# A changed order of steps, and one store for two, at the end of a post-norm attention and feed-forward block

## The chip, the core and the metric

The kernel runs on one core of a Trainium2 chip. The core has a matrix engine (TensorE, PE in the profile), a vector engine (VectorE, DVE), an engine for pointwise functions (ScalarE, ACT), a general one (GpSimd, POOL) and one that mainly starts transfers (SyncE, SP). Each has its own stream of instructions; they wait for each other through semaphores. Transfers run on 16 DMA engines and are started from the streams of SP, ACT or POOL. The metric is the time of one execution on the device in microseconds (us), the median over runs.

## What is computed

4096 tokens of width 256 go through two halves, each followed by a layer norm of the sum with its input:

```python
def _layernorm(x, axis=-1, eps=1e-05):
    m = jnp.mean(x, axis=axis, keepdims=True)
    v = jnp.var(x, axis=axis, keepdims=True)
    return (x - m) / jnp.sqrt(v + eps)

x = L0_attn_x                                   # (1, 4096, 256)
x = _layernorm(x + attention(x))                # linear attention, width 64
x = _layernorm(x + ffn(x))

# ffn: w1, w2 256 -> 1024, h1, h2 1024 -> 1024, w3 1024 -> 256; tlin(x, w, s) = (x @ w.T) * s
h = silu(tlin(x, w1, s1)) * tlin(x, w2, s2)
h = gelu(tlin(h, h1, hs1)); h = gelu(tlin(h, h2, hs2))
return tlin(h, w3, s3)
```

The change is in the very last layer norm, for the last 256 tokens.

## The kernel before

The tokens are cut into eight tiles of 512 (NT = 8); a tile is four groups of 128 tokens (NS = 4), one token to a partition. Tiles are worked on in pairs. Products are made from two roundings of each float32 operand, a high part and a low part, so every weight block is multiplied twice. TensorE runs the products of the feed-forward layers one after the other for the whole program.

The schedule is written by hand: the order of the calls in the source is the order of the instructions on each engine. The framework adds the semaphores.

The kernel takes a short way that holds only for certain weights and variances. While it runs, it gathers tests of that: `differ` compares weights, `within` (lines 1003 to 1006) tests that each group's variance lies between `low` and `high`. At the end all tests are reduced to one number, `flag`. PE, ACT, DVE and SP load it (line 1219), and branch on it (line 1225): where the flag is set, `general` computes everything again in plain float32; otherwise the program ends. On these inputs the branch skips it.

The end of the program, after the last products (lines 1152 to 1225), handles the last pair of tiles, `ta` and `tb`. For each group: `scaled` (line 891) multiplies the product in PSUM by s3 on VectorE, a sum adds it to the residual in `x2`, `bn_stats` and `bn_aggr` on VectorE give mean and variance into `mvo`, a reciprocal root is formed, and the group is normed and stored. The early groups take their root from GpSimd (`rstd_of`, line 84) and are normed by two ScalarE instructions (`norm_on_act`).

The last two groups of `tb`, 2 and 3, are done otherwise. `root_on_act` (line 1133) takes the square root on ScalarE, adds epsilon to the variance on VectorE, and returns four small VectorE steps: a reciprocal and one Newton step in three instructions. In the kernel before, the lines from 1190 run as follows. Group 2: statistics (by `statistics`), root, minus mean, and its subtraction on ScalarE (line 1195). Then VectorE has group 3's scaled product (1196), and group 2's four steps with group 3's sum (1198), statistics (1201) and aggregate (1204) among them. ScalarE scales group 2 (1205), and SP stores it (1206, 128 KB). Group 3: its root (1207), the range tests of `tb` (1208), and its four steps with the minimum over all tests (1210), TensorE's 1x1 product that sums it over the partitions (1213) and the comparison that makes `flag` (1216) among them. VectorE norms group 3 in one instruction (1217), SP stores it (1218, 128 KB), and the flag is loaded.

Of the kernel before, what the change touches and what calls it, by code (L numbers as in the profile page):

```python
# [11 lines left out]
F32 = mybir.dt.float32  # L12
# [3 lines left out]
AF = mybir.ActivationFunctionType  # L16
ALU = mybir.AluOpType
# [4 lines left out]
P = 128  # L22
# [22 lines left out]
def block_kernel(ctx: ExitStack, tc: tile.TileContext, a: dict, out: bass.AP):  # L45
# [15 lines left out]
    nc = tc.nc  # L61
# [3 lines left out]
    def const(name, shape, dt=F32):  # L65
        return cp.tile(shape, dt, tag=name, name=name)

    s1 = const("s1", [P, KH])
# [13 lines left out]
    flag = const("flag", [1, 1], I32)  # L82
# [14 lines left out]
    p2 = fast.enter_context(tc.tile_pool(name="two", bufs=2))  # L97
# [24 lines left out]
    x2 = {}  # L122
# [24 lines left out]
    def norm_stats(us, mv, s0):  # L147
        st = p2.tile([P, 2, 6], F32, tag="bn", name="bn")
        for j, u in enumerate(us):
            nc.vector.bn_stats(st[:, j, :], u)  # L150
        for j in range(len(us)):
            nc.vector.bn_aggr(mv[:, s0 + j, :], st[:, j, :])
# [331 lines left out]
    def sums(layer, k, raw):  # L484
# [20 lines left out]
        def first():  # L505
            plus(v[0], a21, a22)
            plus(v[1], v[0].bitcast(F32), a11, ALU.subtract)
            store(0)

        def second():  # L510
            plus(v[2], a11, a21, ALU.subtract)
            plus(v[3], a12, v[1].bitcast(F32), ALU.subtract)
            store(1)
# [23 lines left out]
    for c in (slice(0, H // 2), slice(H // 2, H)):  # L537
        d = nc.gpsimd.dma_start(out=w1[:, :, c], in_=a["w1"][:, :, c])
# [237 lines left out]
    for i in range(2, 2 * KH):  # L776
# [13 lines left out]
        if i in (11, 14):  # L790
            t = 2 + i // 14
# [86 lines left out]
    mvo = p1.tile([P, NT * NS, 2], F32, tag="mvo", name="mvo")  # L878
# [12 lines left out]
    def scaled(t, s):  # L891
        ps = (al, be)[t % 2][s]
        d = p2.tile([P, E], F32, tag="d", name=f"d{t}", bufs=4)
        nc.vector.tensor_tensor(d, ps[:, :E], s3, ALU.mult)  # L894
        return d
# [28 lines left out]
    def end_jobs(t, engine=nc.gpsimd, queue=nc.gpsimd):  # L924
        root, norm, store = out_norm(t)

        def half(s):
            root([s, s + 1])
            for i in (s, s + 1):
                norm(i, engine)  # L930
            if s:
                store(0, NS, queue)

        return [(1.3, functools.partial(half, s)) for s in (0, 2)]
# [68 lines left out]
    def within(dst, var, so_far):  # L1003

        nc.vector.tensor_scalar(dst, var, low, so_far, ALU.is_ge, ALU.mult)
        nc.vector.scalar_tensor_tensor(dst, var, high, dst, ALU.is_le, ALU.mult)
# [20 lines left out]
    for p in range(NP):  # L1027
        ta, tb = 2 * p, 2 * p + 1
        if p > 0:
            first = []  # L1030
            ask(1)
            for i in range(2 * KH):
# [13 lines left out]
                if p + 1 < NP and i in (6, 11):  # L1046
                    t = ta + 2 + int(i == 11)
# [77 lines left out]
    def statistics(t, ss):  # L1125
        norm_stats([x2[t][:, s, :] for s in ss], mvo[:, t * NS : (t + 1) * NS, :], ss[0])
# [6 lines left out]
    def root_on_act(t, s):  # L1133

        var, r, e = (p3.tile([P, 1], F32, tag=n, name=n) for n in ("var", "rr", "re"))
        mv = mvo[:, t * NS + s, 1:2]
        nc.scalar.activation(r, mv, AF.Sqrt, bias=eps)
        nc.vector.tensor_scalar(var, mv, EPS, None, ALU.add)


        return r, [
            functools.partial(nc.vector.reciprocal, r, r),
            functools.partial(nc.vector.scalar_tensor_tensor, e, r, var, r, ALU.mult, ALU.mult),
            functools.partial(nc.vector.tensor_scalar, e, e, -0.5, 1.5, ALU.mult, ALU.add),
            functools.partial(nc.vector.tensor_tensor, r, r, e, ALU.mult),
        ]

    def store(t, s0, s1):
        nc.sync.dma_start(out=out[t][:, s0:s1, :], in_=x2[t][:, s0:s1, :])

    g, v = nc.gpsimd, nc.vector
    for s in range(NS):
# [23 lines left out]
    for s in range(2):  # L1176
        norm_on_act(ta, 2 + s, *ra[s])
    store(ta, 2, 4)
    d = scaled(tb, 1)
    statistics(tb, [0])  # L1180
    (r0,) = roots(tb, [0])
    y = x2[tb][:, 1, :]
# [6 lines left out]
    store(tb, 0, 2)  # L1189
    n = (NT - 1) * NS  # L1190
    y, u = x2[tb][:, 2, :], x2[tb][:, 3, :]
    statistics(tb, [2])
    r, steps2 = root_on_act(tb, 2)
    (m,) = minus_mean(tb, [2])
    nc.scalar.activation(y, y, AF.Identity, bias=m, scale=1.0)
    d = scaled(tb, 3)
    steps2[0]()
    v.tensor_tensor(u, u, d, ALU.add)
    steps2[1]()
    st = p2.tile([P, 2, 6], F32, tag="bn", name="bn")  # L1200
    nc.vector.bn_stats(st[:, 0, :], u)
    steps2[2]()
    steps2[3]()
    nc.vector.bn_aggr(mvo[:, n + 3, :], st[:, 0, :])
    nc.scalar.activation(y, y, AF.Identity, scale=r)
    store(tb, 2, 3)
    r, steps3 = root_on_act(tb, 3)
    within(ok[:, n - NS :], mvo[:, n - NS :, 1], fine)
    steps3[0]()
    nc.vector.tensor_reduce(some, ok, AX.X, ALU.min)  # L1210
    steps3[1]()
    pf = bank[7][:1, :1]
    nc.tensor.matmul(pf, some, ones, start=True, stop=True)
    steps3[2]()
    steps3[3]()
    nc.vector.tensor_scalar(flag, pf, float(P), None, ALU.is_lt)
    nc.vector.tensor_scalar(u, u, mvo[:, n + 3, 0:1], r, ALU.subtract, ALU.mult)
    store(tb, 3, 4)
    differs = nc.values_load(
        flag, engines=AGAIN, min_val=0, max_val=1,  # L1220
        skip_runtime_bounds_check_because="0 or 1: a comparison's result",
# [177 lines left out]
```

## Time and profile before

| what | us |
|---|---|
| median of 3 runs | 638.11 (638.07 to 639.05) |
| the profiled execution | 637.49 |
| its span, first to last instruction | 635.6 |
| mean granted TensorE clock | 0.997 of full |

The profile comes from one execution on the chip. Its page gives for each engine the busy time and its share of the span, a picture of the span in 40 slices, the DMA queues, the chain of work that ended last, and groups of like instructions. A row of the timeline has the start in us from the span's start, the duration, the engine, the line of the program, the operation, and what it writes and reads. Engine names with a q (SPq, ACTq) are sequencers: they wait, branch, or start transfers, while the engine itself may be idle. Queue 1 in the DMA views is SP's, queue 0 GpSimd's, queue 10 ScalarE's; queues of kind "instruction" bring program code to the engines.

The stores of the last tiles, as their line 1149 shows them (duration ns least, median, largest; first and last start):

```profile
L1149 SPq DMA_DIRECT2D out<-x x5: 332/333/338, 623.3 to 631.9; - x5
```

The first three are of two groups each (256 KB), the last two of one (128 KB).

### The profile page before, as it was taken

What the parts mean: (1) busy time and instruction counts of PE and PEld (TensorE: products, weight loads), DVE (VectorE), ACT (ScalarE), POOL (GpSimd) and SP (SyncE); (2) the same over time, 40 slices, a digit from 0 to 9 for tenths busy, and PEclk for the clock granted to TensorE, in tenths of its full rate; (3) what the DMA queues carried; (4) which work ended last, traced back from release to release, by engine and by line L of the source; (5) the groups of instructions that cost most, each with busy time, mean ns of one, the idle gap of its engine ahead of it and who ended that gap; (6) DMA issues with size and microseconds to landing.
All of it is one profiled execution on the core that took longest, in us unless ns stands there. A gap on an engine that the chain in (4) does not pass through costs nothing.

```text
span 635.6 us, 9039 instructions
## 1 busy us (share of the span) xinstructions
PE 623.6 (98%) x3169; PEld 526.8 (83%) x3169; DVE 488.0 (77%) x767; ACT 379.1 (60%) x547; POOL 218.0 (34%) x280
## 2 busy tenths in 40 slices
PE   8999999999999999999999999999999999999995
PEld 6778888888898888888898888888898888888895
DVE  2889985889568788789668798798676896597456
ACT  5455452659845374655755457757764547765674
POOL 1333023204855409405545505603653700000043
PEclk9999999999999999999999999999999999999998
DMA  8979669978651168646851135645761035543201
GB/s 345 377 270 320 228 218 360 278 248 244 168 154 67 59 206 276 221 134 215 231 151 33 67 131 185 218 162 173 229 162 35 33 131 171 174 153 132 100 1 69
DMA packets 59409, 113.31 MB, mean 178 GB/s; under 512 B 19776, under 2 KB 34112, under 8 KB 59232
## 3 DMA queue, kind: packets, MB, share of 16 engines
q1 hardware_dynamic: 40880, 73.89, 35.7%
q0 software_dynamic: 18192, 38.41, 19.6%
q8 instruction: 26, 0.43, 0.3%
q10 hardware_dynamic: 288, 0.39, 0.2%
q14 instruction: 23, 0.19, 0.1%
HBM read 96.94 MB, written 18.87 MB: 182 GB/s over the span
## 4 chain that ended last, share of the span: by engine, by line
PE 93%; DMA 3%; DVE 2%; issue 0%; ACT 0%; SPq 0%; POOL 0%; DVEq 0%; POOLq 0%
PE bank L305 64%; PE bank L724 18%; PE bank L885 9%; DMA f<-in_h 2%; PE bank L140 1%; DMA f<-in_xt 1%; DVE so L317 1%; PE bank L210 0%; DVE stk L663 0%; DVE bn L150 0%; PE bank L650 0%; PE bank L734 0%; DVE d L894 0%; PE bank L615 0%; ACT hi L218 0%
## 5 line engine op out<-in xcount | busy, mean ns | idle before, releaser
L305 PE MATMUL bank<-hi,ws 128*128 128x512 f32 x896 | 348.7, 389 | 0.0
L305 PE MATMUL bank<-lo,ws 128*128 128x512 f32 x896 | 348.6, 389 | 0.0
L260 DVE TENSOR_TENSOR lo<-f,hi 128x1024 fp32r<-128x1024 f32 x142 | 168.3, 1224 | 59.5 <-ACT hi L259 59.0
L305 PEld LDWEIGHTS bank<-hi,ws 128*128 128x128 f32 x896 | 168.2, 188 | 34.9
L305 PEld LDWEIGHTS bank<-lo,ws 128*128 128x128 f32 x896 | 168.2, 188 | 34.9
L259 ACT CAST hi<-f 128x1024 fp32r<-128x1024 f32 x142 | 142.6, 1052 | 48.4 <-PE bank L305 25.1
L355 ACT ACTIVATE f<-f,hs 128x512 f32<-128x512 f32 x96 | 62.5, 715 | 68.7 <-DVE f L317 68.7
L724 PE MATMUL bank<-hi,w 128*128 128x512 f32 (+1 forms) x256 | 99.0, 388 | 1.0 <-DVE stk L663 1.0
L724 PE MATMUL bank<-lo,w 128*128 128x512 f32 (+1 forms) x256 | 98.8, 387 | 0.0
L743 ACT ACTIVATE f<-bank,s 128x512 f32<-128x512 f32 x64 | 44.0, 689 | 64.8 <-PE bank L724 60.2
L317 DVE TENSOR_TENSOR f<-f,f 128x1024 f32<-128x1024 f32 x64 | 76.5, 1221 | 4.5 <-ACT f L355 3.8
L317 DVE TENSOR_TENSOR f<-f,bank 128x512 f32<-128x512 f32 x96 | 61.4, 681 | 15.3 <-ACT f L410 11.3
L744 DVE SCALAR_TENSOR_TENSOR f<-bank,s,f 128x512 f32<-128x512 f32 x64 | 47.7, 747 | 24.9 <-PE bank L724 23.8
L885 PE MATMUL bank<-w,lo 128*128 128x256 f32 x240 | 57.9, 283 | 0.0
L885 PE MATMUL bank<-w,hi 128*128 128x256 f32 x240 | 57.9, 283 | 0.0
L724 PEld LDWEIGHTS bank<-hi,w 128*128 128x128 f32 x256 | 48.1, 188 | 10.8 <-DVE stk L663 1.2
L244 POOL DMA_DIRECT2D xT<-x x96 | 52.2, 551 | 14.0 <-DMA stage<-in_h 5.9
L724 PEld LDWEIGHTS bank<-lo,w 128*128 128x128 f32 x256 | 48.1, 188 | 9.5
L847 POOL DMA_DIRECT2D stage<-in_h x16 | 9.2, 575 | 126.6 <-DVE stage L873 96.7
L885 PEld LDWEIGHTS bank<-w,lo 128*128 128x128 f32 x240 | 46.1, 192 | 0.2
L885 PEld LDWEIGHTS bank<-w,hi 128*128 128x128 f32 x240 | 46.0, 192 | 0.2
L410 ACT COPY f<-bank 128x512 f32<-128x512 f32 x32 | 18.6, 589 | 28.6 <-PE bank L305 28.5
(165 smaller groups left out, 544.5 us busy)
## 6 DMA issues: line engine op xcount, KB each, us to landing
ws<-sw SPq DMA_DIRECT2D x100, 512.0 KB, 3.5
sw<-so POOLq DMA_DIRECT2D x16, 512.0 KB, 4.9
stage<-in_h POOLq DMA_DIRECT2D x16, 512.0 KB, 5.5
ws<-in_h POOLq DMA_DIRECT2D x12, 512.0 KB, 6.3
sw<-in_h SPq DMA_DIRECT2D x12, 512.0 KB, 5.6
x<-in_x SPq DMA_DIRECT2D x16, 256.0 KB, 5.2
f<-in_xt SPq DMA_DIRECT2D x7, 512.0 KB, 6.7
f<-in_h SPq DMA_DIRECT2D x6, 512.0 KB, 7.2
```

The lines of the kernel that those rows point to most:

```text
L244: moves.popleft()()
L259: nc.scalar.copy(hi[:, c, :], src[:, c, :])
L260: nc.vector.tensor_tensor(lo[:, c, :], src[:, c, :], hi[:, c, :].bitcast(F32), ALU.subtract)
L305: nc.tensor.matmul(ps[2 * h + o], w[:, k, o * P : (o + 1) * P], part[i][:, k, :], start=start and k == 0 and i == 0, stop=k == HK - 1 and ...
L317: engine.tensor_tensor(dst, u, v, op)
L355: nc.scalar.activation(dst, src, AF.Gelu, scale=sc[:, o : o + 1])
L410: nc.scalar.copy(bb[:, o], al[o])
L724: nc.tensor.matmul(ps[:, c], w[:, k, o * P : (o + 1) * P], part[:, 2 * j + k, c], start=(k == 0 and i == 0), stop=(k == KE - 1 and i == 1),)
L743: nc.scalar.activation(g, pa, AF.Silu, scale=s1[:, o : o + 1])
L744: nc.vector.scalar_tensor_tensor(g, pb, s2[:, o : o + 1], g, ALU.mult, ALU.mult)
L847: nc.gpsimd.dma_start(out=st[:, :n], in_=src.rearrange("p k o -> p (k o)")[:, c : c + n])
L885: nc.tensor.matmul(ps[:, :E], part[q][:, k, s * P : (s + 1) * P], w3[:, k0 + k, :], start=i % 2 == 0 and k == 0 and q == 0, stop=i % 2 == ...
```

## The change

- Group 3's scaled product and sum move ahead of group 2's root, and its statistics ahead of group 2's first small step.
- Group 2's subtraction on ScalarE stays, its scaling now comes after the flag's comparison in the source.
- The range tests, the minimum and the 1x1 product move ahead of most of the small steps; the flag's comparison moves ahead of the last step of group 2 and the last two of group 3.
- The small steps of groups 2 and 3 alternate. Group 2 gets a `bn` buffer of its own in place of that in `statistics`.
- The two stores of 128 KB from SP become one of 256 KB from ScalarE's queue, after both groups are normed.

```diff
-    def store(t, s0, s1):
-        nc.sync.dma_start(out=out[t][:, s0:s1, :], in_=x2[t][:, s0:s1, :])
+    def store(t, s0, s1, queue=nc.sync):
+        queue.dma_start(out=out[t][:, s0:s1, :], in_=x2[t][:, s0:s1, :])
...
     y, u = x2[tb][:, 2, :], x2[tb][:, 3, :]
-    statistics(tb, [2])
+    st2, st3 = (p2.tile([P, 2, 6], F32, tag="bn", name="bn") for _ in range(2))
+    nc.vector.bn_stats(st2[:, 0, :], y)
+
+    d = scaled(tb, 3)
+    nc.vector.bn_aggr(mvo[:, n + 2, :], st2[:, 0, :])
+    v.tensor_tensor(u, u, d, ALU.add)
     r, steps2 = root_on_act(tb, 2)
     (m,) = minus_mean(tb, [2])
     nc.scalar.activation(y, y, AF.Identity, bias=m, scale=1.0)
-    d = scaled(tb, 3)
+    nc.vector.bn_stats(st3[:, 0, :], u)
     steps2[0]()
-    v.tensor_tensor(u, u, d, ALU.add)
-    steps2[1]()
-    st = p2.tile([P, 2, 6], F32, tag="bn", name="bn")
-    nc.vector.bn_stats(st[:, 0, :], u)
-    steps2[2]()
-    steps2[3]()
-    nc.vector.bn_aggr(mvo[:, n + 3, :], st[:, 0, :])
-    nc.scalar.activation(y, y, AF.Identity, scale=r)
-    store(tb, 2, 3)
-    r, steps3 = root_on_act(tb, 3)
+    nc.vector.bn_aggr(mvo[:, n + 3, :], st3[:, 0, :])
+    r3, steps3 = root_on_act(tb, 3)
     within(ok[:, n - NS :], mvo[:, n - NS :, 1], fine)
-    steps3[0]()
     nc.vector.tensor_reduce(some, ok, AX.X, ALU.min)
-    steps3[1]()
     pf = bank[7][:1, :1]
     nc.tensor.matmul(pf, some, ones, start=True, stop=True)
+    steps2[1]()
+    steps3[0]()
+    steps2[2]()
+    steps3[1]()
+    nc.vector.tensor_scalar(flag, pf, float(P), None, ALU.is_lt)
+    steps2[3]()
+    nc.scalar.activation(y, y, AF.Identity, scale=r)
     steps3[2]()
     steps3[3]()
-    nc.vector.tensor_scalar(flag, pf, float(P), None, ALU.is_lt)
-    nc.vector.tensor_scalar(u, u, mvo[:, n + 3, 0:1], r, ALU.subtract, ALU.mult)
-    store(tb, 3, 4)
+    nc.vector.tensor_scalar(u, u, mvo[:, n + 3, 0:1], r3, ALU.subtract, ALU.mult)
+    store(tb, 2, 4, nc.scalar)
```

## The prediction

> **What bounds the kernel now.** I read the page first, then the chain of waits, the timeline of the last microseconds, and the DMA views. The page (busy time by engine, clock row, chain by engine):
>
> ```profile
> span 635.6 us, 9039 instructions
> PE 623.6 (98%) x3169; PEld 526.8 (83%) x3169; DVE 488.0 (77%) x767; ACT 379.1 (60%) x547; POOL 218.0 (34%) x280
> PEclk9999999999999999999999999999999999999998
> PE 93%; DMA 3%; DVE 2%; issue 0%; ACT 0%; SPq 0%; POOL 0%; DVEq 0%; POOLq 0%
> ```
>
> TensorE is the bound, at full clock, and the diff adds no product to it. Its last product ends at 627.8; everything the change touches lies between 627.4 and the span's end. The stretches (length, busy time by engine, clock, DMA share, GB/s) divide that end:
>
> ```profile
> 627.40:629.90 2.50, 0.39 (x4) 0.19 (x2) 2.37 (x12) 1.12 (x4) 0.00 (x0) 1.00 0.28 108
> 629.90:631.90 2.00, 0.19 (x2) 0.09 (x2) 1.76 (x10) 0.67 (x2) 0.00 (x0) 0.98 0.19 66
> 631.90:633.80 1.90, 0.00 (x0) 0.00 (x0) 0.00 (x0) 0.00 (x0) 0.00 (x0) 0.50 0.29 86
> 633.80:635.61 1.81, 0.00 (x0) 0.00 (x0) 0.00 (x0) 0.00 (x0) 0.00 (x0) 0.50 0.02 5
> ```
>
> Up to 631.9 VectorE is nearly always busy and sets the end; then 1.9 us in which only the last store moves, then 1.8 us of barriers. VectorE's last rows (start, us):
>
> ```profile
> 629.70 0.17 DVE L1204 BATCH_NORM_AGGREGATE mvo<-bn 128x2 f32<-128x6 f32 x1
> ...
> 630.79 0.22 DVE L1211 SCALAR_TENSOR_TENSOR re<-rr,var 128x1 f32<-128x1 f32 x1
> 631.05 0.15 DVE L1214 TENSOR_SCALAR re<-re 128x1 f32<-128x1 f32 x1
> 631.24 0.16 DVE L1215 TENSOR_TENSOR rr<-rr,re 128x1 f32<-128x1 f32 x1
> 631.32 0.14 DVE L1216 TENSOR_SCALAR flag<-bank 1x1 int32<-1x1 f32 x1
> 631.44 0.41 DVE L1217 TENSOR_SCALAR x<-x,mvo,rr 128x256 f32<-128x256 f32 x1
> ```
>
> Two rules of spacing come from these rows: a step that needs the step before it starts 0.035 us after that one's end (631.20 to 631.24), an independent one 0.08 us before that end (631.32 against 631.40). The sequencers' rows for the flag's load and the branch (duration ns, start):
>
> ```profile
> L1219 PEldq TENSOR_LOAD <-flag x1: 487/487/487, 631.5 to 631.5; - x1
> L1219 SPq TENSOR_LOAD <-flag x1: 518/518/518, 632.3 to 632.3; - x1
> L1225 SPq EVENT_SEMAPHORE  x8: 17/17/17, 633.4 to 633.9; - x8
> L1225 SPq COMPARE_BRANCH  x1: 70/70/70, 632.8 to 632.8; - x1
> ```
>
> SP issues the last store at 631.88, loads the flag at 632.26, branches, and from 633.36 walks eight DMA semaphores. The store lands at 633.71; its semaphore is the fifth, which SP reaches at 633.73. So landing and SP's own path meet within 0.02 us, and the rest, to 635.61, takes 1.88 us.
>
> **The change, part by part.**
>
> *VectorE's order.* I lay the new order out with the old durations. Statistics of group 2 stay at 627.38 to 627.81. The scaled product of group 3 now comes next and waits for TensorE's last product (627.79): 627.83 to 628.24. Then the aggregate of group 2 to 628.34, the sum of group 3 to 628.70, var and minus-mean to 628.84, statistics of group 3 to 629.17, reciprocal to 629.25, aggregate of group 3 to 629.39 (before: 629.87). ScalarE's second root then runs 629.42 to 629.70, right after its mean subtraction. VectorE goes on with var 629.57, the two range tests 630.03, the minimum 630.24; then the two Newton chains alternate, each step in the other's 0.035 us gap: 630.37, 630.44, 630.54, 630.69; flag 630.75; then 630.82, 630.88, 631.08; last scaling 631.11 to 631.52. Before it ended at 631.85: **-0.33**, and the flag, at 631.46 before, comes **0.71 earlier**. No step is added or dropped. TensorE's 1x1 product (0.19) hides behind the chains, as before.
>
> *Group 2's scaling on ScalarE* waits for 630.82 and for ScalarE: about 630.92 to 631.43, beside VectorE's last steps. It ends 0.09 before group 3's. If that cover went, the store would wait for it.
>
> *The store's queue.* SP began 0.03 after VectorE's end. ScalarE's issue waits for VectorE and its own scaling (and an old DMA semaphore, long met). ScalarE's old scaling, with two such waits, began 0.095 after the later one (629.78 to 629.87). So the issue is at 631.62 against 631.88: **-0.26**. The issue itself is unseen on ScalarE at a quiet time; at the start ScalarE's took 397 ns beside 385 on SP, so I price it like SP's 333; ends -0.02 and +0.1. Behind it on ScalarE wait its flag load (0.47), branch and drain, done near 633.2; POOL's barrier needs that only at 634.84. SP loses two issues (2 x 0.33); neither SP nor ScalarE has another transfer behind them, and POOL issues none in this stretch.
>
> *One store of 256 KB for two of 128 KB.* Rows of before:
>
> ```profile
> out<-x SPq DMA_DIRECT2D x3, 256.0 KB, 2.0
> out<-x SPq DMA_DIRECT2D x2, 128.0 KB, 1.8
> ```
>
> Here a rule and a row part. The Trainium skill (DMA: Bandwidth & Descriptors, Anatomy of one DMA) has a fixed part of about 2.0 us in each transfer (fitted there for GpSimd's path); its rules for kernel authors say to coalesce small ones. Read onto this end, one store fewer saves up to 2 us. The trace says no: the first of the two landed at 632.17, wholly beside the second. What counts is the last landing, which gets longer, 2.02 against 1.83: **+0.19**. I take the row.
>
> *SP's tail.* SP no longer issues, loads the flag at 630.78, branches by 631.44 and stands waiting when the store lands. In the instruction order the store's semaphore is now fourth, with one more walk step (0.07) behind it: **+0.06**. The Trainium skill (Runtime: NRT & Kernel Launch, Instruction fetch mechanics) says that a taken branch whose target isn't in the window stalls until a fetch brings it. By that rule SP's stall, on the path before, would now be hidden, a gain. The trace shows SP at its next instruction 0.445 us after its branch, while its 8 KB fetch only starts 1.02 us after it; there is no such stall. I count nothing.
>
> Sum so far: -0.26 + 0.19 + 0.06 = **0.0**. All the gained time is handed back at the landing.
>
> *What the earlier branch triggers.* The packets after the branch are instruction fetches: 8 KB at 633.12, 16 KB at 633.26 (TensorE's queue), 8 KB at 633.36, 8 KB at 633.94. The store's packets ran 632.71 to 633.23, so the fetches fell just behind them. With the flag 0.71 earlier, SP's fetch comes 1.02 after its branch, at 632.46 (before: 633.94), TensorE's 1.77 after its load, at 632.55, VectorE's about 633.0. The new store's packets start 0.83 after the issue and last 0.83: 632.45 to 633.28. **They now meet.** Two loads of 512 KB with nothing else moving, one without and one with a fetch:
>
> ```profile
> q1 hardware_dynamic: 144, 0.52, 39.4%
> ws<-sw SPq DMA_DIRECT2D x1, 512.0 KB, 3.2
> ...
> q8 instruction: 1, 0.02, 1.4%
> ws<-sw SPq DMA_DIRECT2D x1, 512.0 KB, 3.8
> ```
>
> Quiet loads beside one 16 KB fetch landed at 3.84, 3.86 and 4.76, against 3.2: +0.64, +0.66, +1.56, mean 0.95. In the trace a fetch is one packet that holds one DMA engine, and that engine's last packets straggle. The store needs all its packets, so one late engine delays it. The fetches seem to share an engine: alone 8 KB takes 0.31, at the end 0.61 and 0.64; together 40 KB took 1.49 us. Here 8 + 16 + 8 KB meet the store: by that rate 32 x 1.49 / 40 = 1.2 us; by the loads 0.95 x 2 = 1.9. Ends 0 (another engine, another moment) and 1.9; I take 1.5, between the two estimates. Before had at most 0.07 of it (1.83 against 1.77 for the first 128 KB store).
>
> Total: 0.0 + 1.5 = **+1.5**. The profiled execution took 637.49 (1.89 outside its span); the span becomes 637.1. The median of the runs is 638.11, 0.62 above that execution; I add the difference to it: 638.11 + 1.5 = **639.6**.
>
> **The rivals.** 0.2% is 1.28 us, about what a measurement of this kernel can tell from no change: limits 636.8 and 639.4.
>
> *A: no or little collision.* The fetches come earlier or later, or use another engine, or share kindly: 0.0 to +1.2, so 638.1 to 639.3. For it: the 8 KB fetch at 627.45 hurt nobody, and starts are known to about 0.2 us. Against: the computed times coincide from the first packet.
>
> *B: faster.* SP runs its walk of semaphores and drains ahead of the landing, since it branches 1.5 us earlier. If only the closing barriers, some 0.8 us from 634.8, stood behind the landing, about 1.1 of the 1.88 us would go, with -0.26 more from the issue if the larger store cost nothing: 636.8. It decides only if the landing is waited for last. Against: the order has it fourth, with the walk behind it.
>
> *C: the change doesn't do what it says.* VectorE's chains interleave badly, or ScalarE's scaling (ends 631.43) ends after VectorE's and sets the issue: up to +0.3, 638.4. It stays within A's class.
>
> **The numbers.** Forecast (collision of 1.3 us and more) 0.60, A with C 0.31, B 0.09. A collision near 1.2 lies on the limit, so the class follows its size: slower 0.60, within 0.2% 0.31, faster 0.09. The range takes in A's lower end less 0.2 and the forecast's upper end (+2.0): 637.9 to 640.1; the forecast's own range is 639.4 to 640.1.
>
> **What would show it.** VectorE's last scaling ending near 631.5 and the flag near 630.75 confirm the order. The store from ScalarE should issue near 631.6; a landing 2.0 later is rival A, 3 or more the collision, with stray DMA packets after 633.3 and fetches between 632.4 and 633.1. If SP's walk stood before the landing, B holds. I am wrong if the landing is quick, or if the span moves without it.

## The result, and the profile after

| | before | after |
|---|---|---|
| median of 6 runs | 638.94 us (638.07 to 639.83) | 641.4 us (640.55 to 642.01) |
| profiled execution / its span | 637.49 / 635.6 | 641.46 / 639.6 |

The ratio is 1.0034, with a 95% interval of 1.0021 to 1.0047: the change costs 1.3 to 3.0 us. The page of the changed kernel (span, busy time of TensorE and the others, clock, chain by engine):

```profile
span 639.6 us, 9037 instructions
PE 625.6 (98%) x3169; PEld 528.6 (83%) x3169; DVE 488.2 (76%) x767; ACT 379.1 (59%) x547; POOL 218.9 (34%) x280
PEclk9999999999999999999999999999999999999998
PE 93%; DVE 2%; DMA 2%; SPq 1%; issue 1%; ACT 1%; POOL 0%; ACTq 0%; DVEq 0%; POOLq 0%
```

The same number of products is busy 2.0 us longer. So this span holds two differences, one ahead of the changed lines and one in them. Group 2's statistics, the first instruction of the changed part, start at 627.38 before and at 629.73 after. From there to the end of the span it is 8.22 us before and 9.85 after. I call this stretch **the end**; its growth is **+1.63 us**. The 2.35 us ahead of it lie in code that the change doesn't touch; they are taken up under after_again. Small times of the flag, the stores, their packets and the fetches (3.40, 5.20) count from its start.

VectorE's last rows after the change (start, us):

```profile
632.85 0.22 DVE L1212 SCALAR_TENSOR_TENSOR re<-rr,var 128x1 f32<-128x1 f32 x1
632.99 0.14 DVE L1213 TENSOR_SCALAR flag<-bank 1x1 int32<-1x1 f32 x1
633.05 0.14 DVE L1214 TENSOR_TENSOR rr<-rr,re 128x1 f32<-128x1 f32 x1
633.12 0.14 DVE L1216 TENSOR_SCALAR re<-re 128x1 f32<-128x1 f32 x1
633.29 0.16 DVE L1217 TENSOR_TENSOR rr<-rr,re 128x1 f32<-128x1 f32 x1
633.49 0.41 DVE L1218 TENSOR_SCALAR x<-x,mvo,rr 128x256 f32<-128x256 f32 x1
```

Counted from the start of the end, the last scaling finishes at 4.18 (before 4.47), and the flag at 3.40 (before 4.08). VectorE is 0.29 us earlier. Then the stretches (start:end, length, busy time by engine, clock, DMA share, GB/s):

```profile
632.25:634.00 1.75, 0.19 (x2) 0.09 (x2) 1.55 (x11) 0.51 (x1) 0.00 (x0) 0.88 0.00 0
634.00:637.65 3.65, 0.00 (x0) 0.00 (x0) 0.00 (x0) 0.00 (x0) 0.00 (x0) 0.50 0.25 83
637.65:639.61 1.96, 0.00 (x0) 0.00 (x0) 0.00 (x0) 0.00 (x0) 0.00 (x0) 0.50 0.00 0
```

The stretch in which no engine works and only the store and the code fetches move was 1.9 us and is now 3.65. The rows of the flag's load, the branch and SP's walk of semaphores:

```profile
L1220 SPq TENSOR_LOAD <-flag x1: 478/478/478, 633.2 to 633.2; - x1
L1220 PEldq TENSOR_LOAD <-flag x1: 492/492/492, 633.2 to 633.2; - x1
L1226 SPq EVENT_SEMAPHORE  x8: 17/17/17, 634.2 to 637.9; - x8
```

SP begins its walk at 634.2 and stands at the fourth semaphore, the store's, until 637.6. Why the store takes so long is in the DMA views: the row DMA has the busy share of the DMA engines in 40 slices, a queue's row has packets, MB and busy share, the last row the store's size and its us from issue to landing. First the last 4.1 us before the change, where the last store's packets are one block and the fetches come behind it:

```profile
DMA  9400000000017999083000020000000000000000
out<-x SPq DMA_DIRECT2D x1, 128.0 KB, 1.8
```

Then after the change, the store's first 1.7 us and the 2 us that follow:

```profile
DMA  0000000000000000009079949495959596966204
q10 hardware_dynamic: 128, 0.24, 36.9%
q8 instruction: 1, 0.02, 4.6%
q14 instruction: 1, 0.01, 2.6%
out<-x ACTq DMA_DIRECT2D x1, 256.0 KB, 3.6
...
DMA  0104107102000200200010110101000000000000
DMA packets 18, 0.04 MB, mean 22 GB/s; under 512 B 3, under 2 KB 3, under 8 KB 16
q10 hardware_dynamic: 16, 0.03, 4.5%
```

The store has 144 packets, and each DMA engine ends its share with one of 4 bytes (the three "under 512 B" are those of the last three engines). The packets' records don't name their engine; the shares are told apart by their times. By 635.7 thirteen of sixteen engines are through. Two of the rest finish by 636.19, the last one at 637.14. TensorE's fetch, the 16 KB packet of queue 8, ran from 634.92 to 636.18. Only then, by their times, did the last engine's eight data packets begin, one after the other.

### The profile page after: what moved, and what is told of

Same layout as the page of the kernel before. It is cut to its first block, busy times and chain, and to the rows that moved or that the text cites. A ratio compares the mean times of both kernels' runs of the same rounds, so it can differ in the third digit from the quotient of the medians.

```text
span 639.6 us, 9037 instructions
## 1 busy us (share of the span) xinstructions
PE 625.6 (98%) x3169; PEld 528.6 (83%) x3169; DVE 488.2 (76%) x767; ACT 379.1 (59%) x547; POOL 218.9 (34%) x280
## 4 chain that ended last, share of the span: by engine, by line
PE 93%; DVE 2%; DMA 2%; SPq 1%; issue 1%; ACT 1%; POOL 0%; ACTq 0%; DVEq 0%; POOLq 0%
PE bank L305 63%; PE bank L724 17%; PE bank L885 7%; PE bank L581 1%; PE bank L140 1%; DMA sw<-in_h 1%; SPq L244 1%; PE bank L600 1%; DMA f<-in_xt 1%; PE bank L650 0%; PE bank L210 0%; PE bank L640 0%; DMA xT<-x 0%; DVE d L894 0%; DVE bn L150 0%
## 5 line engine op out<-in xcount | busy, mean ns | idle before, releaser
L900 POOL TENSOR_TENSOR x<-x,d 128x256 f32<-128x256 f32 x29 | 25.7, 905 | 31.7 <-DVE d L894 31.6
```

Source lines behind the costliest of these rows:

```text
L900: engine.tensor_tensor(y[:, s, :], y[:, s, :], scaled(t, s), ALU.add)
```

## The experiments

The end is counted from the start of group 2's statistics to the last instruction; "landing" is from the last store's issue. All figures but the ratios come from one profile of each kernel. (The expectations give 9.88 for the changed kernel's end, from rounded times; 9.85 is from the exact ones.)

| kernel | flag set | last store issued | landing | end | ratio to before, 95% interval |
|---|---|---|---|---|---|
| before | 4.08 | 4.50 | 1.83 | 8.22 | |
| after | 3.40 | 4.25 | 3.63 | 9.85 | 1.0034 (1.0021 to 1.0047) |
| after_again | 3.40 | 4.25 | 4.03 | 10.25 | 1.0030 (1.0019 to 1.0040) |
| sp_queue | 3.40 | 4.24 | 3.98 | 10.18 | 1.0039 (1.0025 to 1.0053) |
| flag_last | 4.22 | 4.24 | 2.12 | 8.34 | 1.0005 (0.9993 to 1.0016) |
| no_branch | 3.39 | 4.25 | 2.07 | 7.47 | 0.9988 (0.9978 to 0.9999) |
| one_store_act | 4.07 | 4.54 | 2.56 | 9.07 | 1.0020 (1.0011 to 1.0030) |
| no_hint | 3.40 | 4.25 | 4.00 | 10.22 | 1.0029 (1.0015 to 1.0044) |
| pe_late | 3.40 | 4.25 | 3.55 | 9.77 | 1.0039 (1.0024 to 1.0054) |
| pe_waits | 3.40 | 4.25 | 2.48 | 8.70 | 1.0008 (0.9996 to 1.0019) |
| two_flag_last | 4.23 | 4.21 | 1.96 | 8.06 | 0.9989 (0.9977 to 1.0000) |
| two_flag_last_again | 4.23 | 4.21 | 1.96 | 8.07 | 0.9999 (0.9985 to 1.0013) |

**sp_queue: is it the queue?**

```diff
-    store(tb, 2, 4, nc.scalar)
+    store(tb, 2, 4)
```

> The changed kernel with its one store issued from SP instead of ScalarE. The end is measured from the start of group 2's statistics on VectorE to the end of the span: 8.22 us before, 9.88 after. Theory (code fetches meet the store): TensorE's 16 KB fetch still comes 1.7 to 1.8 us after the early flag and holds one DMA engine, so the store still needs 3.2 to 3.7 us to land and the end is 9.5 to 9.9. Rival (ScalarE's queue is slow): the store lands in 2.0 us, the end is 8.2 to 8.4, and the time is that of before.

The store from SP is as late as that from ScalarE, 3.98 against 3.63 and 4.03, though later than the 3.2 to 3.7 that were expected: TensorE's fetch took 1.6 us here, 1.26 in the first profile of the changed kernel. The rival that ScalarE's queue is slow falls. In the DMA view of its end queue 1 carries the store now, and the fetch is there again:

```profile
q1 hardware_dynamic: 144, 0.26, 16.5%
q8 instruction: 1, 0.02, 2.2%
out<-x SPq DMA_DIRECT2D x1, 256.0 KB, 4.0
```

SP's own 8 KB fetch, told from the others by the order of the branches, moved from 5.06 to 6.61; TensorE's stayed at 5.19. Here the store's last packet ended 0.95 after that fetch, as in the changed kernel (0.96).

**flag_last: the flag alone moved back.**

```diff
-    nc.vector.tensor_scalar(flag, pf, float(P), None, ALU.is_lt)
     steps2[3]()
...
     nc.vector.tensor_scalar(u, u, mvo[:, n + 3, 0:1], r3, ALU.subtract, ALU.mult)
+    nc.vector.tensor_scalar(flag, pf, float(P), None, ALU.is_lt)
```

> The changed kernel with the flag's comparison put behind the last scaling on VectorE, so that the flag is loaded about 0.8 us later; the store stays on ScalarE's queue. Theory (code fetches meet the store): the fetches now start near the end of the store's packets; it lands in 2.0 to 2.3 us and the end (8.22 before, 9.88 after) is 8.2 to 8.5. Rival (ScalarE's queue, or the larger store, is slow): it lands in 3.6 us and the end stays at 9.8.

Same queue, same size, nearly the same issue; the branches of SP and TensorE come 0.8 us later, and the store lands in 2.12:

```profile
DMA  0000000000499999540420050000000000000000
q10 hardware_dynamic: 144, 0.26, 15.3%
q8 instruction: 1, 0.02, 1.4%
out<-x ACTq DMA_DIRECT2D x1, 256.0 KB, 2.1
```

The store is one closed block, and the fetches stand behind it: the first starts at 5.91, when the last packets end (5.94). 1.5 of the 1.63 us are gone with one line moved.

**no_branch: no fetches at all.** The loads of the flag, the branch and the general path are left out.

```diff
-    differs = nc.values_load(
...
     fast.close()
...
-    with tc.If(differs > 0, label="again"):
-        general(tc, a, out, locals())
```

> The changed kernel without the loads of the flag, the branch and the general path behind it (it leaves out the second computation that a set flag would start). Theory (fetches behind the branch meet the store): without them the store from ScalarE lands in 2.0 us and the end is 8.2 or less. Rival (ScalarE's queue or the store's size): 3.6 us and an end of 9.8, less what the branch itself costs.

```profile
q10 hardware_dynamic: 144, 0.26, 15.4%
out<-x ACTq DMA_DIRECT2D x1, 256.0 KB, 2.1
```

No instruction queue shows in this view, and the landing is 2.07. Against flag_last, where the fetches come behind the store, it is only 0.05 less. The end is 0.87 shorter still: without the branch, SP passes five semaphores between the landing and its closing barriers instead of seventeen.

**one_store_act: the old order, one store.** In the kernel before, `store` gets its `queue` argument, and:

```diff
-    store(tb, 2, 3)
...
-    store(tb, 3, 4)
+    store(tb, 2, 4, nc.scalar)
```

> The kernel before in its old order with the two last stores joined into one of 256 KB from ScalarE's queue. Theory (code fetches meet the store): the flag is set 0.4 us ahead of the last scaling, the fetches of TensorE and VectorE start 1.8 us after it, in the second half of the store's packets, so it lands in 2.2 to 3.2 us and the end is 8.6 to 9.5, between the two kernels. Rival (ScalarE's queue or the size alone): 3.6 us and an end of 10.1; and if neither queue, size nor fetch matters, 2.0 us and 8.4.

It landed in 2.56, with an end of 9.07, inside what the theory gave. The fetches came later than was expected, 2.3 and 2.5 us after the flag instead of 1.8: the first at 6.34, TensorE's at 6.54, as the store's last packet ended. The landing is still 0.49 later than without fetches (2.56 less 2.07); which fetch costs what here isn't shown. Joining the stores alone costs 0.85 us, 0.73 of it in the landing: the store is issued no earlier than before, is twice as large, and its tail meets the fetches. No run has the early flag with two stores of 128 KB, so what the larger store adds to the loss there stays open.

**after_again: the changed kernel once more.**

> The changed kernel once more. Theory (all of the loss is in the end): the end is 9.7 to 10.2 again, the part ahead of it differs from that of before only by when TensorE's clock becomes full, 627.2 to 630.1 in the profiles so far, and the median over more runs is 1.6 to 2.0 us above before. Rival (the change also slows the part ahead of the end): the part ahead of it is at 629.7 again with the full clock early, and the median stays 2.4 to 2.7 above before.

The end was 10.25 this time, just above the 10.2 that was expected: TensorE's fetch took 1.63 us instead of 1.26, and the landing moved with it. In the four profiles with the early flag and the branch as it was (after, after_again, sp_queue, pe_late) that fetch ended at 6.46, 6.82, 6.80 and 6.30. Each time the last share of the store began within 0.06 us of that moment, and the store landed 1.41 to 1.50 us after it.

The stretch ahead of the end took 628.09, with full clock from 4.84 us on; in the first profile it was 629.73, with full clock from 8.93. In the median, 640.66 against 638.88 of before (+1.78), the loss is about that of the end. So the 2.35 us ahead of the end in the first profile are not the change's; sp_queue, with the same lines up to there, began its end at 627.20, earlier than before. In the traces 1.9 of the 2.35 us are there by TensorE's 41st product, and the rest arises between the 801st and the 1201st; what makes that rest isn't known.

**no_hint: the branch without its hint.**

```diff
-    tc.mark_branch_hint_location("again", "LikelyTaken", engines=AGAIN)
```

> The changed kernel without the hint that tells the four sequencers ahead of time where the branch goes. If the hint is what lets them go on at once, the first instruction behind the branch comes later than 0.45 us after it, and SP, ScalarE, VectorE and TensorE stall for their fetch; the fetches then still run beside the store, which lands in 3 us or more, and the end is 9.8 or more. If the fetches are started by the hint, they disappear or move, the store lands in 2.0 to 2.5 us and the end is 8.2 to 9.

The branch's rows (duration ns, start):

```profile
L1225 PEldq COMPARE_BRANCH  x1: 4118/4118/4118, 631.8 to 631.8; - x1
L1225 ACTq COMPARE_BRANCH  x1: 54/54/54, 633.0 to 633.0; - x1
...
L1225 ACTq EVENT_SEMAPHORE  x1: 17/17/17, 635.9 to 635.9; - x1
```

TensorE's branch lasted 4.1 us instead of 0.39. The next instruction came 2.8 us after the branch on ScalarE instead of 0.42, and 3.7 on VectorE instead of 0.53; SP's came 0.14 us after it, so SP's part of the guess failed. The fetches beside the store are there without the hint too, hence the branch and not the hint starts them. The end, 10.22, is about that of after_again: these stalls lie beside the late landing.

**pe_late: a miss.** Six products on TensorE behind the flag's were to delay its branch.

```diff
     nc.tensor.matmul(pf, some, ones, start=True, stop=True)
+    for _ in range(6):
+        nc.tensor.matmul(bank[6], stacks[:, 0, :P], stacks[:, 1, :], start=True, stop=True)
```

> The changed kernel with six more products of 128x512 on TensorE behind the flag's 1x1 product (their result is used nowhere), so that TensorE alone loads the flag and branches 0.9 to 1.4 us later; SP, VectorE and ScalarE branch as in the changed kernel. If TensorE's 16 KB fetch is what holds the store, it now starts behind the store's packets; only SP's 8 KB fetch meets their start, the store lands in 2.2 to 2.8 us, and the end is 8.4 to 9.0, against 9.85 and 10.25 in two profiles of the changed kernel. If each fetch does as much harm, or they all share one engine, the store needs 3.2 us or more and the end is 9.5 or more.

They delayed nothing. The first product starts at 630.85, the last ends at 632.51, yet TensorE's sequencer loads the flag as early as SP's:

```profile
L1222 SPq TENSOR_LOAD <-flag x1: 478/478/478, 631.2 to 631.2; - x1
L1222 PEldq TENSOR_LOAD <-flag x1: 487/487/487, 631.2 to 631.2; - x1
```

The sequencer hands products over and goes on; in this run work in the array didn't hold up its branch, at 631.8. So this run says nothing on the question; it is a third profile of the changed end.

**pe_waits: TensorE's branch made to wait.** A 1x1 product that reads the last scaling makes the sequencer wait for a semaphore.

```diff
+    nc.tensor.matmul(bank[6][:1, :1], u[:, :1], ones, start=True, stop=True)
     store(tb, 2, 4, nc.scalar)
```

> The changed kernel with one 1x1 product on TensorE that reads the last scaling's output (its result is used nowhere), placed ahead of TensorE's load of the flag: it makes TensorE's sequencer wait for the last scaling, so TensorE alone loads the flag and branches about 0.8 us later. If TensorE's 16 KB fetch is what holds the store most, it starts at about 6.0 us, behind the store's packets (5.1 to 5.9 of the end); only SP's 8 KB fetch meets their start, the store lands in 2.2 to 2.8 us, and the end is 8.4 to 9.0. If each fetch does as much harm, the store needs 3.2 us or more and the end is 9.5 or more.

```profile
L1221 SPq TENSOR_LOAD <-flag x1: 478/478/478, 632.4 to 632.4; - x1
L1221 PEldq TENSOR_LOAD <-flag x1: 487/487/487, 633.3 to 633.3; - x1
...
DMA  0000000005799898112026000000000000000000
q8 instruction: 1, 0.02, 1.6%
out<-x ACTq DMA_DIRECT2D x1, 256.0 KB, 2.5
```

Now TensorE loads 0.9 us after SP. Its 16 KB fetch moves from 5.20 to 6.41, SP's stays at 5.07, and the landing falls from 3.63 to 2.48. The other fetches start within 0.03 us of where they did. So TensorE's fetch costs 1.15 to 1.55 us (3.63 and 4.03 less 2.48), and the other fetches 0.36 to 0.41 (2.48 less 2.12 and 2.07). By time the kernel is back at that of before (1.0008).

**two_flag_last: a version without the loss.** flag_last with two stores of 128 KB:

```diff
     nc.scalar.activation(y, y, AF.Identity, scale=r)
+    store(tb, 2, 3)
...
-    store(tb, 2, 4, nc.scalar)
+    store(tb, 3, 4, nc.scalar)
```

> The changed order with the flag's comparison behind the last scaling, and two stores of 128 KB again, group 2 from SP and group 3 from ScalarE. Theory (code fetches meet the store): the fetches come after both stores' packets; the last one lands in 1.8 to 2.0 us and the end is 7.9 to 8.2, at or a little below the 8.22 of the kernel before, so the time is the same as before or up to 0.3 us less. Rival (the fetches matter little and the order itself costs): the end is above 8.5.

> The version with the flag last and two stores of 128 KB, once more, since its first interval ended at no change. Theory (its end is 0.16 us shorter than that of before, 8.06 against 8.22, and nothing else differs): the end is 8.0 to 8.1 again and the median lies 0 to 0.3 us below before. Rival (the first run's 1.3 us were real): 1 us or more below again.

Its end is 8.06 and 8.07, 0.15 us under that of before (8.22), as expected; the 1.3 us of its first median did not come again (639.01 against 638.74). By time it is the same as before. The two profiles of this one program show where such scatter is from. The first rows of its opening products (start, us), then the same in the second profile:

```profile
4.07 1.17 PE L581 MATMUL bank<-wkv,f 128*128 128x128 f32 x8 [0.42 <-DMA f<-in_xt]
5.68 3.50 PE L581 MATMUL bank<-wkv,f 128*128 128x128 f32 x29 [0.44 <-DMA f<-in_xt]
...
4.24 5.06 PE L581 MATMUL bank<-wkv,f 128*128 128x128 f32 x22 [0.59 <-DMA f<-in_xt]
```

37 products are done by 9.2 us in the first, 22 by 9.3 in the second: in the long rows a product takes 0.12 us and 0.23. The record of the full granted clock begins at 4.15 and at 9.72. In the traces the second profile is 2.05 us behind by the 41st product and 2.06 at the last; the end began at 627.35 and 629.41.

## Why the prediction was wrong, and where it was right

The direction and the mechanism held, and the change in the end, +1.5, measured +1.63. The step that failed is the one from this change to a time: it took 638.11 as the base and gave the range no room for scatter. The time, 641.4, lies above the range's top of 640.1.

- *VectorE's order.* Said -0.33 and a flag 0.71 earlier; measured -0.29 and 0.68.
- *The store's queue.* Said -0.26; the issue came 0.24 earlier. ScalarE's issue took 367 ns, within the ends given.
- *Group 2's scaling* stayed hidden: it ended at 633.79, the last one at 633.91.
- *The larger store.* Said +0.19; without fetches 256 KB landed in 2.07 (no_branch) against 1.83, +0.24.
- *SP's tail.* Said +0.06. From landing to the last instruction: 1.90 us before, 1.96 after. The sum without a collision, said to be 0.0, shows in flag_last's end: 8.34 against 8.22.
- *"I take 1.5" for the collision.* It measured 1.56 and 1.96 (3.63 and 4.03 less 2.07): near in the first profile, low in the second, and 1.9 as its upper end was a little too low. The working behind the 1.5 was wrong in part, so its closeness is partly luck. I had the fetches share one engine at one rate ("32 x 1.49 / 40"). By the packets' times, TensorE's 16 KB holds one engine for 1.1 to 1.6 us where the flag is early, and the store's share there follows it; the 8 KB ones hold up other engines, the next of which was done 0.95 us sooner. pe_waits gives 1.15 to 1.55 to TensorE's fetch alone. The third fetch, which I had among the store's packets at 5.6, started at 6.13. The slow load with +1.56 was the better row.
- *"I add the difference to it: 638.11 + 1.5."* This step put the time out of the range. 638.11 was the median of three runs; with six it was 638.94, and the later sets gave 637.71 to 638.88. Single runs of before reach from 637.3 to 641.5. The range had bounds for the change's costs and none for this scatter, which is larger. Of the 1.8 us by which 639.6 fell short, 0.83 is the base (638.94 less 638.11) and 0.13 the end (1.63 less 1.5). With the base put right, the range's top would still be 0.5 short. The remaining 0.83 is not assigned run by run. It lies within the interval of the measurement (1.3 to 3.0 us), and scatter between runs can make it: four of the six runs of after took 641.2 us or more, but only eight of the 18 of after_again, where the change cost 1.78. The profile of after, with its late clock, shows one way to such a run.
- *Rival A* (no collision) is what flag_last shows: made true, it gives no change (638.56 against 638.73). *Rival B* (walk ahead of the landing) fell: SP stood at the fourth semaphore, and the walk came behind it. *Rival C* (the order doesn't work as laid out) fell: the last scaling ended 0.29 earlier.
- *The fetch stall behind a taken branch.* I set the rule of the Trainium skill (Runtime: NRT & Kernel Launch, Instruction fetch mechanics) aside, since SP went on at once. no_hint shows stalls of 2.8 to 4.1 us on TensorE, VectorE and ScalarE where the hint is missing, as the rule has it, and none on SP. The three went on 1.4 us or more after the packets of their fetches had ended; what they waited for in that time isn't shown. With the hint there is no such stall, but the traffic of the fetches remains.

## What to carry to other kernels

Where a program ends in a branch, the code fetches behind it are traffic too: look at when they start, and set the condition so that they start behind the last store, not beside it. Here that took the loss away; it gained nothing over the kernel before. An earlier instruction is no gain in itself; ask what it triggers, and on which engine of the store that falls. And take a range's width from the scatter of the runs as well as from the costs in the sum.

## What was not expected of the hardware

- One code fetch of 16 KB took 0.9 to 1.6 us at the end of the program, by the packets' times on one DMA engine, and a store over all sixteen engines waited for its one delayed share: it landed in 3.6 to 4.0 us instead of 2.1. The order seems to matter the other way too: in flag_last, where the store's packets were first, TensorE's fetch started 1.3 us after its branch ended instead of 0.8. That the store's packets held it up isn't tested.
- TensorE's sequencer passed six products (1.7 us of array time) without waiting; it loaded the flag and branched while they ran (pe_late).
- The record of full clock on TensorE begins 3.7 to 10.2 us from the start over these profiles. In the pair of two_flag_last that is worth 2.05 us. It isn't the only scatter: pe_waits had full clock from 3.75 us on and began its end 1.6 us later than two_flag_last, 1.1 us of which arose between the 501st and the 801st product, for a reason that isn't known.
